# Sparse attention and one graph layer on one core: the dense rows go from 128 to 32 on four column tiles, the other rows of the first block become gathered slots, and stage B gets a new order

## The chip, the cores and the metric

One core of a Trainium2 chip. The metric is the device time of one execution in microseconds (us), as the median of several runs. Before: 1343.06 us, the median of three runs.

## The reference, cut to what matters

x has 2708 rows of 1024, all in fp32. The adjacency matrix has 2708 x 2708 entries, of which few are not zero. A row's number of neighbours (its degree) falls with its index on average.

```python
q, k, v = x @ Wq.T + bq, x @ Wk.T + bk, x @ Wv.T + bv
z = (q @ k.T) / sqrt(1024) * adj
z = where(z == 0, -10000, z)
x = layernorm(x + relu(softmax(z, axis=1) @ v))     # layer 0
x = layernorm(x + adj @ (x @ W1) + b1)              # layer 1
```

## The kernel before

The kernel works only on the neighbours. **Stage A** forms M = Wq^T Wk from transposed weights and y = xM in 22 blocks of 128 rows, and meanwhile VectorE lists every row's neighbours. The rows are then sorted by degree, so that block 0 holds the 128 rows of highest degree and block 21 those with none. **Stage B** does the attention of a block by gathering, for slot j, the j-th neighbour of each of its rows: a dot with y gives the score, softmax weights sum the gathered rows to r, r is transposed ("flip") and projected with Wv; the new row x1 is scattered to memory. **Stage C** sums the gathered x1 of the neighbours and projects with W1.

Block 0 has too many neighbours for slots and is done densely, for all 2708 columns and 128 rows: scores for stage B, and a product with all rows of x (stage B) and x1 (stage C):

```python
SLOTS = [None, 11, 8, 7, 6, 5, 5, 4, 4, 4, 3, 3, 3, 3, 2, 2, 2, 2, 1, 1, 1, 0]
...
gp = es.enter_context(tc.tile_pool(name="g", bufs=15))      # one ring for gathers and dense loads
...
def dense_rows(lT, src):                                    # L498 holds the matmul
    acc = [p_o.tile([P, HALF], F32, name="po") for _ in range(NH)]
    for c, (c0, n) in enumerate(chunks):                    # 22 tiles of up to 128 rows
        xc = gp.tile([P, D], F32, name="g", tag="g")
        ...                                                 # loads of src[c0:c0 + n]
        for h in range(NH):
            nc.tensor.matmul(acc[h], lT[:n, c, :], xc[:n, h * HALF:(h + 1) * HALF],
                             start=(c == 0), stop=(c == NC - 1))
    ...
# stage B: block 0 comes fifth, heavy and light blocks take turns; stage C begins with block 0
```

## Time and profile before

| | before |
|---|---|
| time | 1343.06 us (1342.81 to 1347.31) |
| stage A, to the end of y's last block | 474.2 us |
| stage B, to the end of the last projection with Wv | 474.2 to 964.9: 491 us |
| stage C and tail | 964.9 to 1342.9: 378 us |
| TensorE, VectorE busy | 90%, 57% |
| bytes moved by DMA | 241.2 MB |

A stage ends where TensorE's last matmul of its kind ends in the timeline. The prediction shows the lines on which the reading of this kernel rests: TensorE full but for three holes.

### The profile page before, as it was taken

To read this page: it belongs to the slowest core of one execution; us is meant where nothing else is said; L and a number is where in the kernel's file an instruction comes from. 1 tells how busy PE (TensorE), PEld (TensorE's weight loads), DVE (VectorE), ACT (ScalarE), POOL (GpSimd) and SP (SyncE) were. 2 spreads that over 40 slices of the span, in tenths; PEclk is the share of its full clock that TensorE was granted. 3 is DMA by queue.
4 is the path that set the end of the run, shared out by engine and by line. 5 is a ranking of instruction groups with operands and counts; after the bars stand their busy time and mean duration, and the time that the engine had idled before them with its cause. 6 is when DMAs were issued, how large, how long until landed. Compare 5 with 4: busy or idle time off the path is not lost.

```text
span 1342.9 us, 9718 instructions
## 1 busy us (share of the span) xinstructions
PE 1210.0 (90%) x3172; PEld 569.0 (42%) x3172; DVE 759.6 (57%) x1314; ACT 229.0 (17%) x640; POOL 426.6 (32%) x360
## 2 busy tenths in 40 slices
PE   6999979999999959069999989999789999999995
PEld 4544434344444424034444434444334444444442
DVE  5899999911111103892698877876204445456721
ACT  2300101232121100110022212223001111111010
POOL 1000000002400003421665554532125875667510
PEclk7899989999999969579999999999989999999998
DMA  9444485432322188476766565641196765667610
GB/s 361 158 152 150 165 296 192 122 94 64 103 64 74 54 290 286 146 238 221 252 224 227 195 207 176 195 166 49 63 363 237 238 203 173 207 232 267 202 47 34
DMA packets 87852, 241.23 MB, mean 180 GB/s; under 512 B 11248, under 2 KB 34128, under 8 KB 84956
## 3 DMA queue, kind: packets, MB, share of 16 engines
q0 software_dynamic: 38336, 137.70, 30.8%
q1 hardware_dynamic: 46392, 91.72, 20.2%
q10 hardware_dynamic: 3064, 11.09, 2.1%
q8 instruction: 27, 0.44, 0.1%
q14 instruction: 33, 0.27, 0.1%
HBM read 207.04 MB, written 33.46 MB: 179 GB/s over the span
## 4 chain that ended last, share of the span: by engine, by line
PE 52%; DVE 21%; issue 11%; DMA 10%; POOL 5%; ACT 1%; SPq 0%; POOLq 0%; ACTq 0%; DVEq 0%
PE po L377 26%; PE po L250 17%; DMA g<-in_x_dram,tabs 7%; DVE few L234 4%; DVE junk L229 4%; DVE a L231 4%; POOL g L349 4%; PE po L498 3%; PE mm L460 3%; DVE junkv L411 2%; DVE r L432 2%; PE tr L368 2%; PE tr L176 1%; DMA g<-y_d,tabs 1%; POOL rstd L391 1%
## 5 line engine op out<-in xcount | busy, mean ns | idle before, releaser
L250 PE MATMUL po<-m_sb,xt 128*128 128x512 f32 x704 | 305.5, 596 | 11.4 <-DMA xt<-in_xT_dram 11.4
L377 PE MATMUL po<-wv_sb,rT 128*128 128x512 f32 x704 | 309.8, 599 | 0.0
L377 PE MATMUL po<-w_sb,rT 128*128 128x512 f32 x672 | 292.0, 592 | 0.0
L349 POOL DMA_INDIRECT g<-in_x_dram,tabs x99 | 130.6, 1319 | 286.1 <-PE tr L131 120.3
L250 PEld LDWEIGHTS po<-m_sb,xt 128*128 128x128 f32 x704 | 134.4, 191 | 180.5 <-issue 170.6
L377 PEld LDWEIGHTS po<-wv_sb,rT 128*128 128x128 f32 x704 | 133.9, 193 | 161.1 <-issue 159.4
L377 PEld LDWEIGHTS po<-w_sb,rT 128*128 128x128 f32 x672 | 126.0, 190 | 150.8 <-issue 149.2
L349 POOL DMA_INDIRECT g<-x_d,tabs x99 | 105.1, 1062 | 68.5 <-issue 28.0
L308 POOL DMA_INDIRECT tab_d<-rec,pos_i x22 | 21.3, 970 | 329.4 <-DVE pos_i L295 323.1
L251 DVE TENSOR_TENSOR yo<-po,y_bc 128x512 f32<-128x512 f32 (+1 forms) x44 | 29.9, 685 | 157.1 <-PE po L250 151.0
L411 DVE SCALAR_TENSOR_TENSOR junkv<-g 128x1024 uint8<-128x1024 f32 x77 | 94.0, 1221 | 33.0 <-DMA g<-in_x_dram,tabs 32.2
L204 PE MATMUL po<-wk_o,wq_o 128*128 128x512 f32 x256 | 112.6, 599 | 0.0
L368 PE MATMUL tr<-ident,r 128*128 128x128 f32 x336 | 47.1, 285 | 60.8 <-DVE r L432 47.2
L432 DVE SCALAR_TENSOR_TENSOR r<-g,pr,r 128x1024 f32<-128x1024 f32 x77 | 98.5, 1280 | 0.7 <-ACT r L430 0.4
L369 ACT ACTIVATE rT<-tr 128x512 f32<-128x512 f32 x86 | 46.8, 591 | 300.5 <-PE tr L368 287.8
L613 DVE SCALAR_TENSOR_TENSOR t<-po,g 128x512 f32<-128x512 f32 x42 | 28.9, 687 | 115.6 <-PE po L377 115.6
L257 ACT ACTIVATE junka<-xt 128x128 f32<-128x128 f32 x176 | 54.5, 309 | 232.5 <-DMA xt<-in_xT_dram 191.1
L592 DVE SCALAR_TENSOR_TENSOR r<-g,valid,r 128x1024 f32<-128x1024 f32 x57 | 79.6, 1396 | 1.1
L391 POOL TENSOR_TENSOR rstd<-ve,negh 128x1 f32<-128x1 f32 (+1 forms) x44 | 34.8, 790 | 142.4 <-DVE ve L389 141.1
L368 PEld LDWEIGHTS tr<-ident,r 128*128 128x128 f32 x336 | 40.7, 147 | 85.3 <-issue 65.6
L387 ACT ACTIVATE junks<-t,lnm 128x1024 uint8<-128x1024 f32 (+1 forms) x44 | 50.5, 1148 | 134.7 <-DVE lnm L385 134.7
L204 PEld LDWEIGHTS po<-wk_o,wq_o 128*128 128x128 f32 x256 | 48.7, 192 | 58.4 <-issue 57.9
(157 smaller groups left out, 978.8 us busy)
## 6 DMA issues: line engine op xcount, KB each, us to landing
a<-in_adj_dram SPq DMA_DIRECT2D x21, 1354.0 KB, 5.8
xt<-in_xT_dram SPq DMA_DIRECT2D x21, 512.0 KB, 4.9
y_d<-yo ACTq DMA_DIRECT2D x21, 512.0 KB, 5.0
xm<-in_xT_dram SPq DMA_DIRECT2D x20, 512.0 KB, 10.8
g<-in_x_dram SPq DMA_DIRECT2D x20, 512.0 KB, 4.4
g<-x_d SPq DMA_DIRECT2D x20, 512.0 KB, 10.2
wq_i<-in_wqT_dram SPq DMA_DIRECT2D x8, 512.0 KB, 6.1
wk_i<-in_wkT_dram SPq DMA_DIRECT2D x8, 512.0 KB, 10.2
```

The lines of the kernel that those rows point to most:

```text
L204: nc.tensor.matmul(po, wq_o[:, o, i * P:(i + 1) * P], wk_o[:, o, hs], start=(o == 0), stop=(o == DC - 1))
L229: nc.vector.tensor_scalar(junk[:n], a[:n], 0.0, None, op0=ALU.not_equal, op1=ALU.add, accum_out=cnt[:n, b:b + 1])
L231: nc.vector.scalar_tensor_tensor(a[:n], a[:n], 1.0, iota[:n], op0=ALU.is_equal, op1=ALU.mult)
L234: nc.vector.max(few[:n, i * 8:(i + 1) * 8], a[:n, cuts[i]:cuts[i + 1]])
L250: nc.tensor.matmul(po, xt[:, c, :], m_sb[:, c, hs], start=(c == 0), stop=(c == DC - 1))
L257: nc.scalar.activation(junka[:, :P], xt[:, c, :], AF.Copy, accum_out=xs[:, c, b:b + 1])
L349: nc.gpsimd.indirect_dma_start(out=g[:n], out_offset=None, in_=src, in_offset=bass.IndirectOffsetOnAxis(ap=tabs[:n, b, word:word + 1], axi ...
L368: nc.tensor.transpose(tr[:, k, :], r[:, c * P:(c + 1) * P], ident)
L377: nc.tensor.matmul(po, rT[:, c, :], w[:, c, h * HALF:(h + 1) * HALF], start=(c == 0), stop=(c == DC - 1))
L411: nc.vector.scalar_tensor_tensor(junkv[:n], yg[:n], scale, xg[j][:n], op0=ALU.mult, op1=ALU.mult, accum_out=s[:n, j:j + 1])
L432: nc.vector.scalar_tensor_tensor(r[:n], xg[j][:n], pr[:n, j:j + 1], r[:n], op0=ALU.mult, op1=ALU.add)
L592: nc.vector.scalar_tensor_tensor(r[:n], xg[j][:n], valid[:n, b, j:j + 1], r[:n], op0=ALU.mult, op1=ALU.add)
```

## The change

Only the 32 rows of highest degree ("hub") stay dense. The 128 columns of the array take them as four column tiles of 32: tile g works on columns 677 g to 677 g + 676 of the adjacency matrix, and the four partial results are added when they are transposed. The other 96 rows of block 0 get 23 slots, done in pieces of 8, each with a softmax that carries on from the last. Lists hold 24 neighbours, not 16. The dot of x with u, part of the score, moves from stage B to stage A and is stored beside y. Stage B begins with block 21, then the three blocks of one slot, which need no y. The last scaling of a layer norm moves from VectorE to ScalarE. The core of the diff, cut:

```diff
-SLOTS = [None, 11, 8, 7, ...]
+SLOTS = [23, 11, 8, 7, ...]
+PIECE = 8
+HUB = 32
...
 def y_block(b):
+    xn = xa.tile([P, D], F32, name="xn")
+    load_rows(xn, x, r0, n)
...
+    yo = xa.tile([P, YW], F32, name="yo")
+    nc.gpsimd.memset(yo[:, D:YW], 0.0)
+    nc.vector.scalar_tensor_tensor(junkc[:n], xn[:n], 1.0, u_bc[:n], ..., accum_out=yo[:n, D:D + 1])
...
-def dense_rows(lT, src):
+def hub_rows(lT, src):
     acc = [p_o.tile([P, HALF], F32, name="po") for _ in range(NH)]
-    for c, (c0, n) in enumerate(chunks):
-        xc = gp.tile([P, D], F32, name="g", tag="g")
+    for k, (c0, n) in enumerate(hub_chunks):                 # 6 groups
+        xc = []
+        for g in range(G):                                   # of 4 tiles
+            xc.append(gp.tile([P, D], F32, name="g", tag="g"))
+            load_rows(xc[g], src, g * GW + c0, n)
         for h in range(NH):
-            nc.tensor.matmul(acc[h], lT[:n, c, :], xc[:n, ...])
+            for g in range(G):
+                gs = slice(g * HUB, (g + 1) * HUB)
+                nc.tensor.matmul(acc[h][gs], lT[:n, k, gs], xc[g][:n, ...])
...
+order = last + single[::-1] + [17, 16, 15, 0, 14, 1, 13, 2, 12, 3, 11, 4, 10, 5, 9, 6, 8, 7]
+jobs = [17, 0, "hub", 16, 0, 15, 0, "one", 14, 1, "one", 13, 1, "one", 2, 12, ...]   # VectorE's order
...
-order = [0] + ...                                            # stage C
+order = [20, 19, 18, 17, 0, 16, 1, 21, 15, 2, 14, 3, ...]
```

The gather ring still has 15 buffers. W1 used to be loaded at the end of stage A; now its place is free only when the columns of x for the dense scores ("xm" tiles) have gone, and it is loaded early in stage B.

## The prediction

> **What bounds the kernel now.** I cut the span by stage first, since its averages mix three limits. Stage A (two flipped weight matrices, their product M, y = xM for 22 blocks, the list of neighbours) runs to 475 us, stage B (attention, then the product with Wv) to 965, stage C (sum of neighbours, the product with W1) to 1326; then a tail of 17. The table by stretch of time has engine busy times, then TensorE's granted clock, the DMA share and GB/s:
>
> ```profile
> 150.00:235.00 85.00, 76.55 (x187) 34.61 (x186) 84.86 (x106) 12.30 (x53) 0.00 (x0) 0.94 0.63 225
> 235.00:475.00 240.00, 237.08 (x560) 105.35 (x558) 59.64 (x129) 54.99 (x273) 21.35 (x22) 1.00 0.28 80
> 475.00:535.00 60.00, 43.12 (x128) 21.88 (x126) 11.51 (x21) 5.14 (x11) 14.19 (x14) 0.83 0.89 310
> 535.00:600.00 65.00, 18.98 (x44) 9.06 (x44) 56.88 (x88) 8.24 (x13) 25.76 (x17) 0.63 0.59 184
> 600.00:900.00 300.00, 286.70 (x775) 135.37 (x775) 225.09 (x461) 58.05 (x112) 149.04 (x121) 0.98 0.64 209
> ```
>
> TensorE (the first busy figure) is full nearly everywhere: the kernel is bound by the sum of its matmuls plus a few holes. VectorE (the third) is full only in 150-235, beside a full TensorE, and has 75% in stage B. Next, TensorE's own timeline shows the holes, as the idle time in brackets and its releaser:
>
> ```profile
> 491.66 1.94 PE L368 MATMUL tr<-ident,g 128*128 128x128 f32 x8 [16.55 <-DMA g<-y_d,tabs]
> ...
> 506.74 27.93 PE L460 MATMUL mm<-xm,rT 128*128 128x512 f32 x76
> 581.02 1.94 PE L368 MATMUL tr<-ident,r 128*128 128x128 f32 x8 [46.35 <-DVE r L432]
> ...
> 977.92 40.27 PE L498 MATMUL po<-g,aT 128*128 128x512 f32 x88 [12.89 <-DMA g<-x_d]
> ```
>
> So between A and B TensorE first waits for a gather of y, then does the dense scores of 128 rows, then waits 46 us while VectorE prepares an 11-slot block. Last, the rows of groups with the unit costs:
>
> ```profile
> L432 DVE SCALAR_TENSOR_TENSOR r<-g,pr,r 128x1024 f32<-128x1024 f32 x77 | 98.5, 1280 | 0.7 <-ACT r L430 0.4
> L411 DVE SCALAR_TENSOR_TENSOR junkv<-g 128x1024 uint8<-128x1024 f32 x77 | 94.0, 1221 | 33.0 <-DMA g<-in_x_dram,tabs 32.2
> L460 PE MATMUL mm<-xm,rT 128*128 128x512 f32 x80 | 37.2, 622 | 0.0
> L498 PE MATMUL po<-g,pT 128*128 128x512 f32 x80 | 34.8, 592 | 0.0
> ```
>
> Mean durations of matmuls overlap; their spacing is what counts. In the chain that ended last, 32 of them (one block's projection) take 13.73-13.74 us, so one costs 0.429 us. Blocks follow each other every 14.61 us, with their 8 transposes.
>
> **What the Trainium skill says.** "TensorE: Matmul & The Clock Gate", Part 3, reports 2.38x for three concurrent 32-column matmuls of 512 columns. No run here shows column tiles yet. Its Part 1 says that an idle array falls back to half clock; the trace agrees: after the 46 us hole the clock averages 0.63, and transposes after the 16.55 us wait take 424 ns instead of 272-285. "VectorE: DVE Perf Modes", the errata section, gives (N+151)/0.96 ns for an fp32 two-operand add: 1224 ns at N = 1024; the trace has 1221 for L411. I use it for the new widths. "DMA: Bandwidth & Descriptors", "Issuing engines are not separate DMA queues", says that loads from different engines share the same 16 DMA engines; the trace agrees: the y gather issued at 479.4 us beside the dense loads took 12.15 us, where gathers in stage B mostly take 5 to 6, and 978-1030 runs at share 1.00 and 360 GB/s.
>
> **The change, part by part.**
>
> *Stage A.* TensorE's work stays. VectorE gets more. Per list: two more range maxima with the fixed part of that row (329 ns at 169 columns, 672 at 508, so some 158 fixed): 0.32 us; three instead of two top-8 rounds on 48 instead of 32 values: about 0.5. 22 lists x 0.85 = 19 us. Per y block a dot with u moves here from stage B: 22 x 1.25 = 27 us, of which perhaps a third falls into the full stretch; the larger sort about 5. VectorE's full stretch then ends some 28 us later. TensorE feels this only through the loads of xt that come behind the adjacency loads (waits of 8.5 and 2.9 us now); I give it 5 us: A ends at 480.
>
> *Dense part on TensorE, removed:* scores 80 x 0.429 + 16 x 0.124 = 36.3 us; two products of 88 x 0.429 = 37.8 each. *Added:* scores as 8 x 2 x 4 source matmuls of 338 or 339 columns; each fp32 matmul is two in the trace (704 = 22 x 16 x 2), so 128 x 0.284 = 36.4 us in a row; each product 6 x 2 x 4 x 2 = 96 x 0.429 = 41.2 in a row. Thus the instructions saved by fewer rows are spent on four tiles, and all gain is concurrency. Since a source matmul's two halves use the same tile and stand next to each other in an in-order stream, I choose a factor of 2 rather than 4: 18 + 20.6 + 20.6 = 59 against 112, a saving of 53.
>
> *The entry to B.* The first four blocks need no y: 4 x 14.6 = 58 us of TensorE work, with the wv weights already loaded, over the y gather and the first attention. The holes of 16.6 and 46.4 vanish, 63 us, with 3 us of cold clock.
>
> *VectorE in B.* Dots: 97 slots (23 + 74) and 3 checks x 1.25 = 125. Accumulation: 1.21 each, the first of every block on ScalarE: 82 x 1.21 = 99. Small operations of 21 pieces, 1.2 each: 25. Three rescalings of r: 3. Ends of 22 blocks (0.68 + 0.68 + 1.3 + 0.3, the last scaling moved to ScalarE): 65. Dense softmax on 677 columns and copies: 7. Sum 324. It cannot start in earnest before y has landed, at 480 + 14 = 494. With 93% filling it ends at 494 + 348 = 842; the last block's flip and projection bring 858. TensorE alone: 480 + 22 x 14.61 (321) + 18 + 21 + 2 = 842. The two are level, so B's last projection ends at 858 (before: 965).
>
> *DMA in B.* (97 + 3 slots + 22 own rows + 21 y) x 0.524 MB = 75, scatters 11.5, scores 11, product 11: 109 MB in 380 us, 287 GB/s. At 326 GB/s per full share (209/0.64) that is 88%: not the bound, but no reserve.
>
> *Stage C.* The end of the last block took 9.3 us from 964.75 to the load at 974.1; one more operation on GpSimd and a ScalarE scaling instead of VectorE's make 10.5: C starts at 869. It now begins with a gather, an accumulation and a flip, about 8 us, no better than the direct load's 3.8. Three blocks (44 us) follow; then comes the block with the dense rows: 9 + 24 + 3 gathers and a load of 11 MB, 30 MB, 87 us at 350 GB/s, against 8 + 44 + 21 = 73 of work. So a stall of some 14 us: block 0 goes on at 869 + 87 = 956. 18 blocks x 14.61 = 263, tail 17: 1236. Rounding up for lost time between: **1238 us**.
>
> **Rivals.**
> *Column tiles do not overlap.* For it: half of each pair must wait for the other, and no trace here shows overlap. Against: the skill's figure. B and C each grow by some 18-20 us, partly under waits: about 1265. A full factor of 4 would give B 20 us on TensorE, but VectorE would then set its end: about 1225.
> *VectorE becomes the bound of B.* For: 324 us of work level with TensorE's 362, and 75% filling in the present stage B, where waits for gathers break it. Against: it is not needed more now, and the pieces and the order are laid out to fill it. At 80%, B ends at 494 + 405 + 16 = 915 and the time is about 1295.
> *The gathers are the bound.* For: 88% share, 15 buffers, and the 360 GB/s ceiling at the start of C. Then the first 100 us of both B and C stretch, 20 to 30 us in all: 1265.
> *Stage A is delayed by the lists.* If the 28 us pass on in full: 1260.
> *The check fails and the dense fallback runs:* over 2000 us; nothing speaks for it, as the capacities grow.
>
> **Range and chances.** The removed holes (63) and a part of the dense saving are nearly certain, which alone gives about 1260; the rivals push up by 20 to 55 and rarely together, full concurrency and a smooth C pull down by 15 to 30. So 1200 to 1280. To miss 2% (1316) nearly all rivals must come at once: faster 0.94, same 0.03, slower 0.03.
>
> **What would show it.** Right: no TensorE hole over 5 us near 475-500; VectorE at 85% or more from 500 to 840; 128 score matmuls in 15 to 25 us and 96 product matmuls in about 21, with spacing near 0.21; the last Wv projection ending near 858; a wait for DMA before the dense matmuls of C, with share near 1.0 there; blocks every 14.6 us afterwards. Wrong: spacing 0.43 (no overlap) or 0.11 (full); blocks of stage B spaced 17 us or more with waits for VectorE; y blocks of stage A ending later than 490; a hole at the start of C of more than 35 us.

## The result, and the profile after

| | before | after |
|---|---|---|
| time | 1344.67 us (1342.81 to 1347.31) | 1365.28 us (1362.93 to 1368.29) |
| stage A ends | 474.2 | 493.6 |
| stage B ends | 964.9 | 945.3 |
| stage A, B, C and tail by themselves | 474, 491, 378 | 494, 452, 416 |
| TensorE, VectorE busy | 90%, 57% | 88%, 59% |
| bytes moved by DMA | 241.2 MB | 275.8 MB |

The ratio after to before is 1.0153, with a 95% interval of 1.0121 to 1.0185: under 2%, but on the slow side. (Ratios here are the mean time of one kernel's fast runs over that of the other's in the same rounds, so not quite the ratio of the medians.) Stage B did get 39 us shorter; stage A took 19 us of that back and stage C 38.

The table by stretch of time of the kernel after, in stage B and at the head of C (length, then busy time and instructions of TensorE, its weight loads, VectorE, ScalarE, GpSimd; then TensorE's granted clock, DMA share, GB/s; a packet counts in full where it starts, so a share can pass 1):

```profile
520.00:560.00 40.00, 36.52 (x200) 15.97 (x201) 24.52 (x39) 7.79 (x14) 19.07 (x16) 0.90 1.02 415
560.00:620.00 60.00, 54.61 (x143) 25.67 (x142) 47.94 (x95) 16.18 (x30) 30.99 (x26) 0.94 0.69 236
620.00:690.00 70.00, 53.43 (x169) 18.85 (x168) 22.59 (x47) 9.86 (x22) 18.94 (x21) 0.87 0.84 240
690.00:750.00 60.00, 31.41 (x83) 15.01 (x82) 54.61 (x108) 12.00 (x20) 40.10 (x34) 0.76 0.79 267
1010.00:1080.00 70.00, 52.05 (x149) 16.10 (x150) 19.53 (x28) 5.92 (x8) 32.47 (x27) 0.81 0.96 287
```

The entry works: TensorE is full from 520 to 560. But in 620 to 690, where the prediction had VectorE filled to 93%, it is busy for 22.59 of 70 us, and in the next stretch it is VectorE that is full and TensorE half empty. The head of stage C looks like 620 to 690 again. TensorE's own timeline there (start, duration, line, output and inputs, shapes, count; in brackets the idle time before it and its releaser):

```profile
633.78 3.58 PE L607 MATMUL po<-g,pT 112*32 112x512 f32 x8 [7.78 <-DMA g<-in_x_dram]
637.29 1.13 PE L419 MATMUL po<-wv_sb,rT 128*128 128x512 f32 x2
638.35 1.90 PE L607 MATMUL po<-g,pT 112*32 112x512 f32 x4
640.18 1.99 PE L419 MATMUL po<-wv_sb,rT 128*128 128x512 f32 x4
642.10 1.92 PE L607 MATMUL po<-g,pT 112*32 112x512 f32 x8
...
669.55 5.34 PE L607 MATMUL po<-g,pT 112*32 112x512 f32 x36
683.55 3.62 PE L403 MATMUL tr<-same,part 128*128 128x32 f32 x16 [8.66 <-DVE part L610]
...
747.40 3.73 PE L410 MATMUL tr<-ident,r 128*128 128x128 f32 x16 [28.59 <-DVE e L460]
```

L607 is the dense product, L419 the projection of another block. The order in which TensorE gets them is fixed when the kernel is compiled, and it wove the product, load by load, between the matmuls of one projection. Read the counts against the times. Four matmuls (one column tile, two halves of the columns, each matmul standing twice in the trace) take 1.90 us; eight (two tiles) take 1.92 too. The tiles do run side by side, but only where more than one of them stands there, and in most of the woven turns one stood alone.

What the other engines did meanwhile, first VectorE, then GpSimd:

```profile
652.61 0.69 DVE L521 TENSOR_TENSOR t<-po,bias_bc 128x512 f32<-128x512 f32 x1 [16.24 <-PE po L419]
669.66 0.69 DVE L521 TENSOR_TENSOR t<-po,bias_bc 128x512 f32<-128x512 f32 x1 [16.36 <-PE po L419]
...
673.43 0.56 POOL L433 TENSOR_TENSOR rstd<-ve,negh 128x1 f32<-128x1 f32 x1 [33.77 <-DVE ve L431]
```

VectorE waits 16 us twice for the woven projection. GpSimd stands 33.77 us at a small operation that waits for VectorE, with its next gathers behind it. Between 610.67 and 677.17 it issued no gather of x at all; then the VectorE work of the next block begins late, and TensorE waits 28.59 us for it at 747.

Last, the groups that answer for stage A, TensorE's, GpSimd's and VectorE's (busy time, mean ns, then idle time before and its main releaser):

```profile
L279 PE MATMUL po<-m_sb,xt 128*128 128x512 f32 x704 | 312.2, 606 | 23.0 <-DMA xt<-in_xT_dram 23.0
L271 POOL MEMSET yo<- 128x4 f32 x22 | 2.2, 102 | 267.4 <-DMA y_d<-yo 205.7
L272 DVE SCALAR_TENSOR_TENSOR junkc<-xn,u_bc 128x1024 uint8<-128x1024 f32 (+1 forms) x22 | 26.9, 1224 | 92.6 <-POOL yo L271 72.0
```

The dot costs VectorE 26.9 us as predicted, but VectorE also waited 72.0 us at it for a memset of GpSimd, and that one for the store of an earlier block of y. TensorE's waits for xt doubled, from 11.4 to 23.0 us.

### The profile page after: what moved, and what is told of

Its sections match the earlier page's. It is cut to its first block, busy times and chain, and to the rows that moved or that the text cites. A ratio compares the mean times of both kernels' runs of the same rounds, so it can differ in the third digit from the quotient of the medians.

```text
span 1361.2 us, 10176 instructions
## 1 busy us (share of the span) xinstructions
PE 1195.5 (88%) x3225; PEld 542.9 (40%) x3225; DVE 802.4 (59%) x1448; ACT 284.2 (21%) x697; POOL 503.5 (37%) x494
## 5 line engine op out<-in xcount | busy, mean ns | idle before, releaser
L419 PE MATMUL po<-wv_sb,rT 128*128 128x512 f32 x704 | 317.8, 607 | 1.7 <-DVE rT L657 1.7
L419 PE MATMUL po<-w_sb,rT 128*128 128x512 f32 x672 | 303.4, 607 | 17.1 <-DVE t L737 17.1
L419 PEld LDWEIGHTS po<-wv_sb,rT 128*128 128x128 f32 x704 | 134.0, 195 | 170.0 <-issue 164.7
L419 PEld LDWEIGHTS po<-w_sb,rT 128*128 128x128 f32 x672 | 127.8, 194 | 177.6 <-issue 162.4
L381 POOL DMA_INDIRECT g<-in_x_dram,tabs x122 | 151.0, 1238 | 96.7 <-issue 46.1
L721 DVE SCALAR_TENSOR_TENSOR r<-g,valid,r 128x1024 f32<-128x1024 f32 x79 | 126.5, 1602 | 66.9 <-DMA g<-x_d,tabs 65.2
L381 POOL DMA_INDIRECT g<-x_d,tabs x122 | 140.8, 1154 | 34.4 <-issue 29.9
L439 DVE SCALAR_TENSOR_TENSOR junkv<-yg,g 128x1024 uint8<-128x1024 f32 x100 | 122.3, 1223 | 31.0 <-DMA g<-in_x_dram,tabs 30.2
L436 ACT ACTIVATE t<-t,nmr,rstd 128x1024 f32<-128x1024 f32 (+1 forms) x44 | 54.6, 1240 | 144.8 <-POOL nmr L435 140.4
L272 DVE SCALAR_TENSOR_TENSOR junkc<-xn,u_bc 128x1024 uint8<-128x1024 f32 (+1 forms) x22 | 26.9, 1224 | 92.6 <-POOL yo L271 72.0
L249 DVE MAX8 few<-a 128x8 f32<-128x75 f32 (+3 forms) x132 | 76.9, 614 | 0.1
L521 DVE TENSOR_TENSOR t<-po,bias_bc 128x512 f32<-128x512 f32 (+1 forms) x44 | 30.2, 686 | 75.4 <-PE po L419 75.4
```

What stands on the lines that cost most here:

```text
L249: nc.vector.max(few[:n, i * 8:(i + 1) * 8], a[:n, cuts[i]:cuts[i + 1]])
L381: nc.gpsimd.indirect_dma_start(out=g[:n], out_offset=None, in_=src, in_offset=bass.IndirectOffsetOnAxis(ap=tabs[:n, b, word:word + 1], axi ...
L419: nc.tensor.matmul(po, rT[:, c, :], w[:, c, h * HALF:(h + 1) * HALF], start=(c == 0), stop=(c == DC - 1))
L436: nc.scalar.activation(t[:n], t[:n], AF.Identity, bias=nmr[:n], scale=rstd[:n])
L439: nc.vector.scalar_tensor_tensor(junkv[:n], yg[:n, :D], scale, xg[:n], op0=ALU.mult, op1=ALU.mult, accum_out=s)
L721: nc.vector.scalar_tensor_tensor(r[:n], xg[:n], valid[:n, b, j:j + 1], r[:n], op0=ALU.mult, op1=ALU.add)
```

## The experiments

Theories: (1) the moved dot delays stage A; (2) the product's loads, which share the ring of 15 buffers with the gathers, keep GpSimd from gathering ahead, so that VectorE starves; (3) the weaving costs TensorE time; (4) the DMA engines are full and late. Rivals are named in what was expected. Eighteen kernels ran, each beside the kernel before, whose median there was 1344.87 to 1346.8 us; all passed the comparison with the reference, even the two that leave out data on purpose (it concerns 32 rows of 2708). "A ends" and "B ends" are the ends of y's last block and of the last projection with Wv in the profiled run; B is the time between, C and tail what follows.

| run | median us | ratio to before, 95% | A ends | B ends | B | C and tail |
|---|---|---|---|---|---|---|
| after | 1365.28 | 1.0153 [1.0121, 1.0185] | 493.6 | 945.3 | 452 | 416 |
| own_b | 1345.62 | 0.9997 [0.9976, 1.0019] | 492.6 | 926.4 | 434 | 416 |
| pin | 1353.72 | 1.0044 [1.0015, 1.0073] | 493.2 | 937.4 | 444 | 416 |
| nodot | 1341.26 | 0.9964 [0.9947, 0.9981] | 476.4 | 931.4 | 455 | 414 |
| entry | 1360.71 | 1.0127 [1.0093, 1.0161] | 491.7 | 943.3 | 452 | 413 |
| fewload (wrong result) | 1314.3 | 0.9783 [0.9747, 0.982] | 493.3 | 897.0 | 404 | 414 |
| clate | 1363.45 | 1.0127 [1.0099, 1.0155] | 494.5 | 948.7 | 454 | 418 |
| combo1 | 1331.5 | 0.9899 [0.9871, 0.9928] | 476.6 | 905.9 | 429 | 425 |
| combo2 | 1323.72 | 0.9849 [0.9825, 0.9874] | 475.2 | 902.8 | 428 | 418 |
| own_l10 | 1381.48 | 1.0255 [1.0238, 1.0273] | 493.5 | 963.4 | 470 | 415 |
| mixb | 1327.83 | 0.9862 [0.9846, 0.9879] | 476.3 | 907.8 | 431 | 414 |
| mixc_l10 | 1363.46 | 1.0125 [1.0108, 1.0142] | 477.0 | 947.7 | 471 | 414 |
| skip_b | 1340.39 | 0.9955 [0.9936, 0.9973] | 479.9 | 915.5 | 436 | 424 |
| skip_c | 1343.36 | 0.9984 [0.9967, 1.0001] | 478.4 | 917.1 | 439 | 424 |
| skip_cc | 1343.44 | 0.9968 [0.9941, 0.9995] | 479.8 | 920.7 | 441 | 424 |
| spread_b | 1321.87 | 0.9845 [0.9812, 0.9878] | 479.0 | 915.5 | 436 | 404 |
| spread_bc | 1326.05 | 0.9848 [0.9828, 0.9868] | 477.1 | 910.3 | 433 | 414 |
| spread_bcc | 1334.22 | 0.9936 [0.989, 0.9982] | 476.2 | 915.0 | 439 | 413 |
| spread_few (wrong result) | 1305.23 | 0.9698 [0.9667, 0.9728] | 478.7 | 897.7 | 419 | 406 |

The kernel before has 491 for B and 378 for C and tail. Some expectations count stage C from its first transposes, some 15 us after B's last projection.

### own_b: buffers of its own for the product in stage B

```diff
+def room_b():                      # the xm tiles are free once the scores are done
+    if not spare:
+        t = xm_pool.tile([P, N], F32, name="xm")
+        spare.extend([t[:, D:2 * D], t[:, :D]])
+    return spare.pop()
...
-            xc.append(gp.tile([P, D], F32, name="g", tag="g"))
+            xc.append(room())      # room_b in stage B, the ring in stage C
```

> Only the 24 loads of the dense product of stage B leave the ring of 15 gather buffers; they go into the three large tiles that held the columns of x for the scores. Ring theory (the dense loads fill the ring, so the next gathers wait, VectorE starves at 636-682 us and TensorE 50 us later): the VectorE holes of 16 + 16 + 8 us in that stretch and the TensorE hole of 28.6 us near 720-747 go, and the time falls by 25 to 35 us, to about 1335. DMA theory (the 16 DMA engines are the limit in that stretch, whoever owns the buffers): the holes stay within 10 us of what they are, and the time stays within 8 us of 1365. Order theory (the gathers stand on GpSimd behind the end of a block whose projection is woven into the product): the holes shrink only if the compiled order changes with the buffers; if GpSimd still waits over 30 us for that block's end before it issues the gathers, this theory holds instead of the ring theory.

It took 19 us off. Between 600 and 690 us GpSimd issued 25 gathers of x, against 13. The stretch in question, by engine, and the hole that was 28.59 us:

```profile
620.00:690.00 70.00, 52.26 (x139) 13.59 (x137) 43.54 (x79) 11.15 (x22) 32.48 (x30) 0.95 1.02 309
```

```profile
722.39 1.94 PE L410 MATMUL tr<-ident,r 128*128 128x128 f32 x8 [8.17 <-DVE r L487]
```

VectorE's busy time nearly doubled to 43.54 of 70 us, and GpSimd no longer stands for 33.77 us. So taking the product out of the ring helps, but the edit moves more than the buffers. The dense loads begin at 545.1 us instead of 610.7, and W1's 4 MB are issued at 684.7 instead of 554.4. GpSimd's order, fixed at compile time, is another too: after the end of a block at 637.79 nine gathers of x stand in front of the next block's end, where the changed kernel has none. So the order theory (that order, and not buffers that ran out, kept the gathers back) is not ruled out; no run separates the two. The gain stayed below what was expected, and the DMA share went from 0.84 to 1.02: the transfers now fill what the buffers had kept empty.

### pin: the product in one piece

```diff
-xc = []
-for g in range(G):
-    xc.append(...)
+xc = [None] * G
+for g in reversed(range(G)):
+    xc[g] = (...)
...
-nc.tensor.matmul(acc[h][gs], ...)
+tc.keep_in_program_order(nc.tensor.matmul(acc[h][gs], ...))
```

> The dense product's matmuls are kept in program order and of each group of four loads the one used first is traced last, so the four column tiles of a group are issued next to each other; the ring stays. Weaving theory (the compiled order follows each single load, so that two halves of one column tile stand alone between full-width matmuls, and their concurrency is lost): the product's 96 matmuls in each of B and C take 15 to 20 us of TensorE instead of some 33, spacing 0.15-0.2 us, and the time falls by 10 to 20 us in all, if TensorE's time is what is short there. Ring theory: TensorE is not short there, VectorE still starves for some 40 us in B, and the time falls by less than 8 us.

It took 12 us off. The product's matmuls fell from 27.7 us to 17.0 in stage B, and GpSimd's longest wait for VectorE there from 33.8 us to 22.1, but TensorE now stands still for the loads, 21.3 us in all, where it had woven in other work. Two of the six groups:

```profile
634.95 3.64 PE L608 MATMUL po<-g,pT 112*32 112x512 f32 x16 [10.94 <-DMA g<-in_x_dram]
644.71 1.92 PE L608 MATMUL po<-g,pT 112*32 112x512 f32 x16
```

Sixteen matmuls on four tiles take 1.92 us, as long as four on one tile: full concurrency. The same sixteen take 3.64 us after a wait of 10.94. That agrees with the Trainium skill, "TensorE: Matmul & The Clock Gate", "Why this matters for your kernels", which warns that gaps of more than some 3 us halve the clock. So pinning pays twice for each wait.

### nodot: stage A without the dot

```diff
-xn = xa.tile([P, D], F32, name="xn")
-load_rows(xn, x, r0, n)
...
-nc.vector.scalar_tensor_tensor(junkc[:n], xn[:n], 1.0, u_bc[:n], ..., accum_out=yo[:n, D:D + 1])
-nc.gpsimd.tensor_tensor(yo[:n, D:D + 1], yo[:n, D:D + 1], beta[:n], ALU.add)
```

> Stage A without the loads of x rows and without the 22 dots with u; the place for the dot holds zero. The dot is the same for all neighbours of a row, so softmax does not see it, and the result should stay right. Dot theory (these dots and loads make the y blocks late: VectorE waits for the y buffer before each dot, and the loads stand in front of the loads of the transposed x on one queue): the last y block ends at 475 to 482 us instead of 493.6, TensorE's waits for that load fall from 23 to about 11 us, and the time falls by 12 to 18 us. List theory (the six ranges and 24 places make the lists longer, and that alone delays the loads): the last y block still ends after 487 us and the time falls by less than 7.

It took 24 us off, more than expected. Stage A ends at 476.4 and TensorE's waits for xt are down to 8.4 us, though the longer lists are all still there: they cost stage A 2 us at most (474.2 before), and the dot with its loads nearly everything. Stage B takes as long as in the changed kernel (455 us against 452); it just starts earlier. The result stays correct, as the term is the same for all neighbours of a row and a softmax doesn't see it (apart from the test for zero, which made no difference in the comparison).

### entry: another place for the first gather buffers

```diff
+wk_o = wa.tile([P, DC, D], F32, name="wk_o", tag="wb")
 wq_i = wa.tile([P, DC, D], F32, name="wq_i", tag="wa")
...
-wk_o = wa.tile([P, DC, D], F32, name="wk_o", tag="wb")
```

> The two weight tiles of stage A swap places, so that the first eight gather buffers of stage B lie over weights that are free from 155 us on, and not over the matrix that TensorE reads until the end of stage A. Place theory (the first gathers of rows of x wait for the end of stage A because of where their buffers lie, so blocks 20 to 18 are late and the dense scores come second): the seven gathers are issued before 480 us, the y gather comes some 8 us earlier after the end of A, TensorE's 10.2 us wait for it shrinks to under 4, and the time falls by 5 to 12 us. Order theory (GpSimd's gathers stand behind something else, or the order of TensorE is fixed by the compiler's own estimate): the gathers still begin at the end of A, and the time stays within 4 us.

It took 4.6 us off, nearly nothing. One gather came earlier (471.64); the next was issued at 492.52, when stage A was over, as before. What GpSimd waited for there the trace doesn't name. Inconclusive.

### fewload: one group of loads for six

own_b, and:

```diff
-    xc = []
-    for g in range(G): ...load...
+    if k == 0 or room is not room_b:      # a wrong result, on purpose
+        xc = []
+        for g in range(G): ...load...
```

> Gives a wrong result on purpose. own_b, and beside it stage B's product reads its first group of four row tiles once and uses it for all six groups, so that about 9 MB of loads (20 of 24) fall away in the stretch 622 to 685 us, where own_b's trace showed the DMA engines busy over their whole time at 302 GB/s. If the transfers took the place of the missing buffers in own_b: about 9 MB at 302 GB/s are 30 us of transfers, some 20 of them felt; the product stretch of 62 us falls to about 40, the DMA share there to about 0.85, stage B's last projection ends 15 to 25 us earlier than own_b's 926, and the run takes 1320 to 1332 us (own_b 1346). Rival, the weaving of the product between full-width matmuls and VectorE's own work set that stretch: under 8 us earlier, 1338 us or more.

It took 31 us less than own_b, 29 of them in stage B, more than expected. But the groups of TensorE show that two things had changed (fewload, then mixb, told below, whose product is woven like own_b's):

```profile
L625 PE MATMUL po<-xm,pT 112*32 112x512 f32 x80 | 8.8, 594 | 0.1
```

```profile
L618 PE MATMUL po<-xm,pT 112*32 112x512 f32 x80 | 25.9, 598 | 4.7 <-DMA xm<-in_x_dram 4.6
```

With its data there, the compiler set the product in one piece: all 96 matmuls in 10.51 us. So fewload took away transfers and weaving together (and W1's load moved from 684.7 to 631.0) and couldn't decide between them; spread_b and spread_few were made for that.

### clate: block 0 later in stage C

```diff
-order = [20, 19, 18, 17, 0, 16, 1, 21, 15, 2, 14, 3, 13, 4, ...]
+order = [20, 19, 18, 17, 16, 15, 14, 0, 13, 12, 1, 11, 2, 21, ...]
```

> The changed kernel; only the order of the blocks in stage C differs: block 0 (the one with the dense rows) comes eighth and not fifth. Theory: the 24 loads of C's product and its gathers share one ring, so VectorE starves for some 34 us in 1045 to 1074 us however far on block 0 stands; a later place moves the starvation but doesn't remove it, and blocks with few neighbours, whose sums take VectorE little, stand in front instead of heavy ones: 1355 to 1367 us (changed kernel 1365), the starved waits of VectorE still 25 us or more in sum. Rival: C's product waits because stage B's last rows come late, and three blocks more in front hide it: 1340 to 1352 us, the waits under 12 us in sum.

The time is within the noise of the changed kernel (1363.45 against 1365.28), and VectorE's waits for gathers at the head of stage C stay (56 us against 53). That speaks against the rival: the loss there doesn't come from rows that are late.

### combo1, mixb, combo2: do the parts add up?

combo1 is nodot, pin and own buffers in B and C (C's over Wv, which is done with); mixb is nodot and own_b alone; combo2 is combo1 with clate's order.

> nodot, pin and own buffers for the product in stages B and C together (C's loads lie over a weight that stage C no longer needs). If the three losses lie behind each other, they add up: 1365 - 24 - 12 - 19 = 1310, and own buffers in C take 10 to 20 more: 1290 to 1310 us; stage B's last projection ends at 880 to 900 us. If they share one limit (the DMA engines full at 302 GB/s between 600 and 690 us), own_b and pin don't add up: 1315 to 1335 us, and stage B's last projection ends after 905 us.

> nodot and own_b together, without pin and with the gather ring in C as it was. combo1 (1331.5) fell 21 us short of the sum of its parts; its trace shows PE waiting 37 us at the pinned product for loads, with the DMA engines full. If the two parts nodot and own_b draw on different losses (end of stage A; stage B's ring), they add up: 1365 - 24 - 19 = 1322, 1317 to 1327 us, that is under combo1, and pinning is what cost combo1 its gain. If the full DMA engines already swallow nodot's earlier start (what begins 17 us earlier waits for the same bytes), 1330 to 1342 us.

> combo1 with clate's order in stage C. If with buffers of its own the C product still stands in the way of VectorE or waits for rows, the later block 0 gains 5 to 15 us over combo1. If combo1 has taken that loss away already, the two are equal within 4 us.

mixb came to 1327.83, about the sum of its parts (1322). combo1, with more in it, was no faster: 1331.5. Stage B ends at 905.9 in one and at 907.8 in the other, with quite different TensorE lines (combo1, then mixb):

```profile
620.00:690.00 70.00, 34.56 (x133) 13.88 (x132) 47.74 (x93) 11.65 (x22) 34.78 (x31) 0.71 1.02 344
```

```profile
620.00:690.00 70.00, 52.68 (x141) 19.19 (x141) 40.42 (x83) 11.89 (x22) 29.74 (x27) 0.93 1.03 344
```

One waits for loads with TensorE idle for half of the stretch, the other weaves and keeps it busy; the DMA engines are full in both, and the end is the same. So TensorE's time isn't what counts there, once the product has buffers of its own. combo2 gained 8 us over combo1, 7 of them in stage C and its tail by the profiled runs.

### own_l10 and mixc_l10: block 0 later in stage B

own_b, or nodot with own buffers in B and C and clate's order, and:

```diff
-order = last + single[::-1] + [17, 16, 15, 0, 14, 1, 13, 2, 12, 3, 11, ...]
+order = last + single[::-1] + [17, 16, 15, 14, 1, 13, 2, 12, 3, 0, 11, ...]
```

> own_b, with only the place of block 0 in stage B's order of projections changed: tenth and not fourth after the single-slot blocks, so that its product's 24 loads fall where the DMA engines have room (own_b's windows: share 1.02 in 620 to 690 us, 0.78 to 0.81 in 690 to 850, 0.30 in 850 to 950). If the transfers in 622 to 685 us are what fewload saved (its last projection of stage B ended at 897 us, own_b's at 926), then moving them, with no byte less, gains most of that: stage B's last projection ends at 898 to 912 us and the run takes 1317 to 1332 us (own_b 1346). Rival, the sum of bytes of the whole of stage B counts and not where they fall, or full-width matmuls lose by the weaving wherever it stands: 1340 us or more.

> All that helped, without pin: nodot, own buffers in B and C, block 0 later in B (tenth) and in C (eighth). If the losses are the dot in A (24), the ring in B (19), the crowded transfers in B (15 to 29) and C's product (8 to 20), the sum is 1365 - 66 to 92: 1273 to 1300 us, stage B's last projection at 875 to 895 us. If clearing one only hands the wait to the next (VectorE, filled by then to 75% in 520 to 850 us, or the gathers of stage C), 1305 to 1325 us.

Both lost some 36 us against the same kernel with the old order (mixc_l10's nearest is mixb). I had moved the projection but not VectorE's work: it still did block 0's 23 slots early, and what TensorE was now to project came after them. own_l10, first the stretch, then the hole:

```profile
620.00:690.00 70.00, 34.11 (x81) 15.33 (x79) 63.11 (x127) 13.96 (x26) 49.66 (x44) 0.77 0.80 271
```

```profile
695.01 3.73 PE L410 MATMUL tr<-ident,r 128*128 128x128 f32 x16 [33.65 <-DVE z L457]
```

With VectorE filled to 90%, TensorE had half of the stretch to itself: where gathers come in time, VectorE is the bound. The rival that it is "the weaving wherever it stands" isn't shown by this; the run is a plain mistake of order.

### skip_b, skip_c, skip_cc: fewer bytes

The dense rows never use what block 0's slots gather for them. Here they stand in the last 32 partitions, and slots are gathered for the 96 others only:

```diff
+nc.sync.dma_start(out=tabs[:P - HUB, 0], in_=tab_d[HUB:P, :])
+nc.sync.dma_start(out=tabs[P - HUB:, 0], in_=tab_d[:HUB, :])
...
-J, n = SLOTS[b], rows[b]
+J, n = SLOTS[b], rows[b] if b else P - HUB
```

skip_b is this on mixb; skip_c has clate's order as well, skip_cc also own buffers in C.

> mixb, and the 32 dense rows of block 0 stand in its last 32 partitions, so that the slots of block 0 are gathered, in stages B and C, for its other 96 rows only: 23 x 32 rows x 4 KB = 3.0 MB less in each stage, no other work changed, result correct. (The dense rows never use what is gathered for them.) If bytes bind stage B between 500 and 690 us, 3.0 MB at the 344 GB/s that mixb's window showed are 9 us: stage B's last projection ends at 895 to 902 us (mixb 908), and as stage C's first 100 us show a DMA share of 0.81 to 0.96 too, it gains some 5 us more: 1312 to 1321 us (mixb 1327.8). If not bytes but the number of gathers, their issue, or VectorE (whose instructions take the same time for 96 rows) sets that stretch: within 4 us of mixb.

> skip_b with block 0 later in stage C (clate's order). combo2 gained 8 us over combo1 by it, with the product's own buffers in C; clate alone gained 2 us. If what makes it gain is only own buffers, this is within 4 us of skip_b; if it is the crowded transfers at the head of stage C, 5 to 12 us under skip_b.

> skip_c with buffers of its own for the product in C (over the weight that C no longer needs). If the gather ring still costs in C, 5 to 12 us under skip_c: 1298 to 1310 us, the fastest so far. If C is held by its transfers and by VectorE's sums of neighbours, within 4 us of skip_c.

A miss: 12 us slower than mixb, and the two others no better. In the profiled runs, which lie 17 us apart, 4 us come with stage A, which ends later; stage B is 4 us longer and stage C 9. As the expectation's rival supposed, VectorE takes as long for 96 rows: 1221 ns a dot, against 1224 for 128. Part of the reason is told by the queues (packets, MB, share of the engines' time over the span), mixb's and skip_b's for the gathers and scatters:

```profile
q0 software_dynamic: 44896, 160.96, 35.8%
```

```profile
q0 software_dynamic: 43424, 154.93, 35.2%
```

35.8% of 1322.2 us are 473 us, 35.2% of 1339.2 are 471: 6 MB fewer, 3.7% of the queue's bytes, took hardly less time of the engines. Over all runs it is 465 to 471 us in the three skip runs and 466 to 473 in the others with the changed kernel's gathers. So skip_b didn't remove what it was meant to remove, and it doesn't speak against full DMA engines: their time didn't follow the bytes here. Why gathers of 96 rows take as long as of 128 stays open.

### spread_b, spread_bc, spread_bcc: contiguous without waiting

mixb with clate's order; each of the product's six groups of 16 matmuls is kept whole, as in pin. In stage B each stands behind one of six successive projections; in stage C they follow each other. Block 0 moves to the ninth place, and VectorE's jobs move along:

```diff
+acc = [p_mm.tile([P, HALF], F32, name="mm") for _ in range(NH)]
...
+    if k < HC - 1:
+        yield                          # next group after the next projection
...
-order = ... [17, 16, 15, 0, 14, 1, 13, 2, ...]
+order = ... [17, 16, 15, 14, 0, 13, 1, 2, ...]
-jobs = [17, 0, "hub", 16, 0, 15, 0, "one", 14, 1, "one", 13, 1, ...]
+jobs = [17, 0, "hub", 16, 15, 0, 14, "one", 0, 13, 1, "one", 1, ...]
```

spread_bc spreads the groups in stage C too, spread_bcc with own buffers there.

> mixb with clate's order in C, and stage B's product cut into its six groups of 16 matmuls (four row tiles each), one group after each of six successive projections and kept contiguous, in PSUM banks that are free by then; block 0's projection is therefore ninth in stage B, and its VectorE pieces are moved along, behind blocks 16, 15 and 14. No byte and no matmul is added or taken away. mixb's product in B cost TensorE 33.5 us of matmul time, 11 us of waits for loads and 8 us before the turn of the parts; contiguous and with its loads in (fewload) it cost 10.7, 0.1 and 5. Theory, the cost is the interleaving with full-width matmuls and the waits, not the bytes: stage B's last projection ends at 872 to 885 us (mixb 908) and the run takes 1290 to 1305 us. Rival, the bytes of this stretch bind, so that gathers come late and TensorE waits for VectorE in the product's place (skip_b, own_l10): after 900 us and 1318 us or more.

> spread_b, with stage C's product spread in the same way, one group after each of the projections before block 0, its loads in the gather ring as before. mixb's product in C cost TensorE 36 us of matmul time and 7 us of waits. If interleaving cost it, stage C's 398 us fall by 20 to 28: 1265 to 1285 us. If the ring that loads and gathers share costs VectorE its sums (waits of VectorE for g in that stretch over 20 us in sum), it gains under 10 us over spread_b.

> spread_bc with buffers of its own for the product in C (over the weight that C no longer needs). If the ring still costs, 5 to 15 us under spread_bc; if not, within 4 us of it.

The product worked as intended: 11.8 us of matmuls in stage B (9.6 for the lines below, 2.2 for the last group) against mixb's 33.5. And it gained nothing there: stage B takes 436 us, mixb's 432. TensorE, then VectorE:

```profile
L619 PE MATMUL mm<-xm,pT 112*32 112x512 f32 x80 | 9.6, 598 | 1.4 <-ACT pT L543 1.4
...
629.57 1.97 PE L404 MATMUL tr<-ident,r 128*128 128x128 f32 x8 [17.87 <-DVE r L481]
```

```profile
574.01 1.23 DVE L433 SCALAR_TENSOR_TENSOR junkv<-yg,g 128x1024 uint8<-128x1024 f32 x1 [7.16 <-DMA g<-in_x_dram,tabs]
588.49 1.22 DVE L433 SCALAR_TENSOR_TENSOR junkv<-yg,g 128x1024 uint8<-128x1024 f32 x1 [8.11 <-DMA g<-in_x_dram,tabs]
606.29 1.23 DVE L433 SCALAR_TENSOR_TENSOR junkv<-yg,g 128x1024 uint8<-128x1024 f32 x1 [5.78 <-DMA g<-in_x_dram,tabs]
```

What TensorE saved it now waits for VectorE, and VectorE for gathers of x. With buffers apart, theory 3 falls as a cause for stage B: the weaving filled time that would have been idle. The move of block 0 could hide a gain here, but combo1 against mixb, without that move, says the same. With the ring the weaving did cost: pin took 8 us off stage B.

In stage C, spreading the groups brought nothing (spread_bc 1326.05, spread_bcc 1334.22, both within or above spread_b). But spread_b itself has the shortest C and tail, 404 us against mixb's 414. There block 0 stands later and its product is kept whole; clate and pin, with one of these each, gained nothing in C (418 and 416), and combo2, with both and own buffers in C, took 418. What made the difference is not shown.

### spread_few: the transfers alone

spread_b with fewload's edit, so that 20 loads of 448 KB fall away and the order stays.

> Gives a wrong result on purpose. spread_b, and its product in stage B reads its first group of four row tiles once and uses it for all six groups: 20 loads of 448 KB (9 MB) fewer, and not a matmul, its place or a gather changed. spread_b's product costs TensorE only 12 us, and yet stage B ended at 915.5: TensorE waits for VectorE now (18 and 13 us at 612 and 662), and VectorE for gathers (7, 8 and 6 us between 567 and 606). If the product's loads are what keeps the gathers waiting on the DMA engines, stage B's last projection ends 15 to 29 us earlier (887 to 900) and the run takes 1293 to 1308 us (spread_b 1321.9). If VectorE's own order of work or the gathers' issue sets that stretch, within 6 us of spread_b.

It took 17 us less than spread_b, and stage B ends at 897.7, 18 us earlier with stage A unchanged, inside what the transfers were expected to give. The queue of these loads from 500 to 900 us (packets, MB, share of the DMA engines' time), spread_b, then spread_few:

```profile
q1 hardware_dynamic: 4872, 22.22, 17.0%
```

```profile
q1 hardware_dynamic: 2330, 13.12, 8.8%
```

The difference is 33 us of the engines' time; about half of it came through to the end. W1's load moved along, from 660.6 to 630.0 us. This was the run that told theories 3 and 4 apart.

## Why the prediction was wrong

The prediction said 1238 us, with 1200 to 1280 as its range; the result is 1365. By the terms of its own sum: A ends 14 us later than its 480; B takes 452 us against 378 (858 less 480), 74 more; the head of C, from B's last projection to the flip of block 0 (1075.0 in the trace), takes 130 against 98 (956 less 858), 32 more; the rest takes 286 against 282. That is the whole difference, 123 us, to the 1361.2 us of the profiled run. By its steps:

**"A ends at 480."** It ended at 493.6. The 27 us of VectorE for the dot were right (26.9), and the longer lists I gave a share of the delay had none. What I left out of the sum is what the dot is tied to: 22 more loads of x, a store that must finish before GpSimd clears the next row of y, and VectorE behind that. Without the dot and its loads (nodot) A ends at 476.4, with the longer lists. The rival "stage A is delayed by the lists" named the wrong cause.

**"I choose a factor of 2 rather than 4."** The tiles overlap in full: 16 matmuls on four tiles in 1.92 us as four on one. The premise failed that the two halves of a tile's matmul stand next to each other and hold up the next tile: in pin's group at 644.71 four matmuls start within 0.02 us, and the next four 0.45 us later. The scores took 12.1 us of matmuls against my 18. The product didn't get it, because it was not in a row as I had assumed: 27.7 us in stage B and 32.1 in C against my 20.6. Yet the size of this term hardly matters in stage B: spread_b cut it to 11.8 us and nothing came of it.

**"The holes of 16.6 and 46.4 vanish."** Mostly right. There remain 10.2 us at the gather of y and 3.1 at the dense scores. In the 106.8 us from the end of stage A on, TensorE is busy for 89.9 us, where before it was 43.9. One reading beside it was wrong: the clock of 0.63 "after the 46 us hole" is the mean from 535 to 600, which holds the hole; in the hole it is 0.54, and after it (581 to 600) 0.85.

**"With 93% filling it ends at 842."** The step that failed with the most weight. The sum of VectorE's work was fair (324 us; it was busy for 301 from 494 to 945), but that fills two thirds of the 451 us. VectorE can work only on what has been gathered, and I took 15 buffers and a good order to be enough. They weren't. I read the profile as a loop of waits that no single row shows: the product's tiles hold the ring, TensorE weaves a projection through the wait for them, VectorE stands in order behind that projection, GpSimd in order behind VectorE, and the gathers behind GpSimd. own_b cuts the loop and takes off 19 us; whether by its buffers or by the order that came with them is not shown.

**"Not the bound, but no reserve."** A mean of 287 GB/s over stage B was a fair figure (269 in 500 to 900), but a mean hides the stretch that counts. Nearly all the dense loads, the 23 slots of block 0, and now W1 fall between 500 and 690 us: the share is 1.02 there as soon as buffers allow it (own_b), at 309 (own_b) to 344 GB/s (mixb). Nor is a full share one rate, as my 326 GB/s had it: from 520 to 560 it went with 415 GB/s. Taking 9 MB of loads away is worth 18 us with the order fixed (spread_few), 29 with the order freed too (fewload). The prediction had quoted that loads and gathers share the same 16 engines, and I used it for the entry only. The rival "the gathers are the bound" had the cause right and its size too small (20 to 30 us for B and C together); the rival of VectorE at 80% filling, 1295 us, named the effect. Stage B's 74 us are these two causes for the most part: with both taken away (fewload, which also leaves out 9 MB of loads that my sum had counted) it takes 404 us, 48 less. What makes up the other 26 is open; 16.5 us of TensorE's waits at the entry are still there in fewload. Counted by TensorE, stage B of the changed kernel is 383 us busy, where my sum had 362, and 69 us idle, where it left 16.

**Stage C.** "A stall of some 14 us" at block 0 became 32 more than the sum had allowed. The trace lists what was new: 15.1 us at the start (`r` of the first block has to be gathered and summed, where the dense product of before needed a wait of 12.9), the product at 32.1 us where I had 20.6, the loads at a DMA share of 0.96. No run got stage C with its tail under 404 us (378 before), neither a later place (clate), nor own buffers (combo1, skip_cc), nor a contiguous product (pin, 17.1 us instead of 32.1 and still 416; spread_bc). No run took C's loads away. So the cause in C isn't settled; the full DMA engines are the suspect, argued from stage B and not shown. From block 0's flip on, blocks follow as predicted.

Several versions beat both kernels: spread_b with 1321.87 us and combo2 with 1323.72 lie 1.5% under the kernel before: less than 2%, but their intervals exclude 1. Both keep the change and add buffers of its own to the product, and drop the dot.

## What to carry to other kernels

When work moves from a dense form to gathered slots, draw up the transfers by stretch and not by stage, and count how many buffers the gathers have left while a burst of loads passes through the same ring. Follow the in-order chain of engines once around (loads, TensorE, VectorE, the engine that issues gathers): if it closes, a wait anywhere in it can stop all of it. And before cutting an engine's busy time, ask whether it was filling a wait: TensorE lost 22 us of work in spread_b, and the end of its stage didn't come earlier.

## What the Trainium skill lacked or had wrong

- "TensorE: Matmul & The Clock Gate", Part 3, gives 2.38x for three column tiles. It has no figure for four. The runs show four fp32 tiles of 32 columns side by side in full: 1.90 us for 4 matmuls on one tile, 1.92 for 16 on four; 96 in 10.51 us.
- "TensorEngine Tiling (Array Packing)", "Key Properties", says that a change of tiling mode drains TensorE, and gives no cost. The woven stretch shows one: four matmuls on a tile start at 638.35 us, four of full width at 640.18, the next on tiles at 642.10. That is 1.83 and 1.92 us, where four in a row take 1.72 (4 x 0.429), so a change there and back costs some 0.3 us.
- No page says what a gather of fewer rows costs the DMA engines: 6 MB fewer in gathers of 96 instead of 128 rows took 471 us of engine time instead of 473 (465 to 471 over three such runs, 466 to 473 over the others).
- No page describes the closed chain by which loads that share a ring with gathers stop the engine that issues the gathers: GpSimd stood 33.77 us at one small operation and issued 13 gathers of x in 90 us, against 25 with buffers apart (and another order).
